# Five batches in the first class of early loads, one allocation for the load buffers, the places' products two steps later, and an adapter down-projection in four blocks

## The chip, the cores and the metric

The kernel runs on one core of a Trainium2 chip, in one launch. The metric is the device time of one execution in microseconds (us). Over 12 executions it was 346.51 us in the median, from 345.58 to 347.81 us. The engines are TensorE (PE in the profile; its weight loads are PEld), VectorE (DVE), ScalarE (ACT), GpSimd (POOL) and SyncE (SP, which here issues most of the DMAs; SPq is its queue).

## The reference

The input `x` has 8 batches of 256 tokens of 128 numbers, all in f32: 2048 tokens, or 16 tiles of 128. There are two layers, each with a residual.

```
# layer 0: a pooling as condition, then 8 experts, all of them computed for every token
scores = tanh(x @ W1 + b1) @ v
p      = softmax(scores masked by the batch's kind)      # up to j / from j / all but j
pooled = (p @ x) / cnt
logits = pooled @ gate_weight.T
gates  = logits * (logits >= the kth smallest of all logits)
x      = x + sum over e of gates[e] * (gelu_tanh(pooled @ w1[e].T + b1[e]) @ w2[e].T + b2[e])
# layer 1: an adapter chosen by the batch's language, then the 2 best of 8 experts
h      = relu(x @ W1[lang] + b1[lang])                   # 128 -> 32
z      = layernorm(x + h @ W2[lang] + b2[lang]) * gamma[lang] + beta[lang]
xn     = layernorm(z) * gamma + beta
w, idx = the two largest of softmax(xn @ gate_w), scaled to sum 1
x      = x + z + sum over the two of w * (gelu(xn @ w1[e] + b1[e]) @ w2[e] + b2[e])
```

## The kernel before

**Units.** The 16 token tiles are cut into five units: units 0 to 2 are full units of four tiles (two batches), units 3 and 4 are half units of two tiles (one batch each). `halves(u)` names the two batches of a full unit, and twice the same batch for a half unit.

**Loading.** SyncE issues, in this order: the input, the first layer's weights `w` (L147, 24 of 256 KB), then for each unit the adapter's weights in loads from L200 on: `lw1` (128 x 32), `lw2` (33 x 129: 32 rows of W2 and a row of b2, with b1 as column 129 of the 32 rows), and `lgb` (gamma and beta). A unit's two `lw2` lie in one tile `las[u]`, at partitions 0 and 64 (`LANE`).

**The pooling.** For batch b, TensorE multiplies the masked weights with the tokens, the gate's columns and a column of ones (`poolp`, L390). VectorE takes the row sums (`rs`, L397), their reciprocal (L398), `pooled` (L400) and the batch's `logit` out of it. Two batches together are turned on TensorE (`poolTp`, L407) and copied by VectorE to `poolT` (L409). Then the first layer's products can start. The order on each engine is settled when the program is built: a planner sorts the operations by its own costs and due times. Those of the beginning (up to L502, on TensorE, VectorE, ScalarE and GpSimd) and of the ending (from L1161, on SyncE too) keep the order of the text among themselves, but an operation from further down in the text may be placed between those of the beginning. A `keep_in_program_order` fixes a single instruction in the same way.

**The first layer.** `layer("first")` goes over the five units and the eight experts. For each, four products `hp_first` (L945) with a GELU on ScalarE each (L947), then, one expert later, four products `yp_first` (L925) into one PSUM tile; VectorE multiplies that with the gates (`part_first`, L913) and adds it up (`acc_first`, L915). Between these products `pump()` advances everything in `behind` by one step: the poolings that remain, the search of the kth value (`threshold`, L531 to L554), and for each finished unit the generator `adapt(u)`. A `yield` in a generator is one step: what follows it is emitted after the next product.

**`adapt(u)`** is the second layer's first half for one unit:

- `x2T`, the residual in turned form (L694); `fp`, the turn back on TensorE; `x` on VectorE (L698);
- `adp`, the down-projection (L705): one product of 32 x (half the unit's tokens) for each of the two lanes, of 256 columns in a full unit, of 128 in a half unit; VectorE adds b1 and takes the relu into `ha` (L707);
- `dp`, the up-projection (L715), one product per tile of 128 tokens, from the two lanes in turn; `xr` adds the residual (L720);
- two layer norms, with GpSimd's `rstd_l` (L582) in them; the turn `znp` (L749); the logits `l1q` and `l1p` (L763, L770, L775);
- the two best experts (`oh1`, `oh2`), the running counts of tokens per expert `sofar` (L802), two steps of pause, and then the places' products `kp` on TensorE (L808, L809), which count for each token its place in its expert's list;
- `at` (L814), the counts of the unit (L817), the counts of a class (`some`, L821), and the scatters of the tokens to DRAM `xs` by GpSimd (L830), then the list of tiles that are full by now.

**The second layer** runs over 36 tiles of 128 rows and, if needed, up to three more. `fetch` issues the loads of weights (`wt`, L983) and tokens (`xt`, L993) some tiles ahead, `turn` turns them (`xtp`, L1019, `xc`, L1021), `hidden` makes the hidden layer (`b`, L1031; `hps`, L1034; `hs`, L1036), `output` the products `yps` (L1043), `yt` (L1047), and scatters the outputs back by GpSimd to `ys` (L1050).

**Classes.** Tiles are taken in an order such that the batches' outputs are complete early for some: class one holds the first `FIRST` = 4 batches, class two those up to `EARLY` = 6. With k the number of a tile, `SETTLED_FIRST` = max(29, 4 x 4 + 7) = 29 and `SETTLED` = 31; at k = 28 `load` fetches the batches of the first class, `yg`, from `ys` (L1069), at k = 30 those of the second. The last two batches are loaded when the loop is over. `add()` adds a batch's two outputs into `resid` (L1076, L1077) and `store` writes it out (L1085). In the ending, three adds and stores stand between the outputs of the last tiles, one more after `brought`, and the rest after all. The outputs of the last four tiles don't go through DRAM: `home` (L1092 to L1099) makes a matrix of places and `brought` (L1106) multiplies it with the outputs into `late`, which VectorE adds at the end (L1182).

Of the kernel before, what the change touches and what calls it, by code (L numbers as in the profile page):

```python
# [10 lines left out]
F32 = mybir.dt.float32  # L11
# [3 lines left out]
ALU = mybir.AluOpType  # L15
# [7 lines left out]
B, S, D = 8, 256, 128  # L23
P = 128
NT = B * S // P
NG = 4
GT = NT // NG
# [3 lines left out]
NU = len(UNITS)  # L31
SLOTS = {2: 17, 3: 21, 4: 39}
E, HC = 8, 4
A = 32
LANE = 64
# [4 lines left out]
NSCR = 15  # L40
# [4 lines left out]
NSLOT = SLOTS[NU - 1]  # L45
SURE = 36
EARLY = 6
FIRST = 4
CLASSES = 3


SETTLED = max(SLOTS[NU - 2] + E, 4 * EARLY + E - 1)
SETTLED_FIRST = max(SLOTS[NU - 2] + E, 4 * FIRST + E - 1)

# [30 lines left out]
def halves(u):  # L85

    g, o, nt = UNITS[u]
    b = (g * GT + o) // 2
    return (b, b + 1) if nt == GT else (b, b)
# [3 lines left out]
def tile_adaln_ffn_d2(ctx: ExitStack, tc: tile.TileContext, x, ptype, lang, cols, b1v,  # L93
                      w10, w20, w11d, w21d, lw1, lw2, lgb, out):
    nc = tc.nc
# [3 lines left out]
    const = ctx.enter_context(tc.tile_pool(name="const", bufs=1))  # L99
    first = ctx.enter_context(tc.tile_pool(name="first", bufs=E))  # L100
    keep = ctx.enter_context(tc.tile_pool(name="keep", bufs=NG))
    work = ctx.enter_context(tc.tile_pool(name="work", bufs=2))
    small = ctx.enter_context(tc.tile_pool(name="small", bufs=4))
    dram = ctx.enter_context(tc.tile_pool(name="dram", bufs=1, space=DRAM))
    psb = ctx.enter_context(tc.tile_pool(name="psb", bufs=4, space=PSUM))
# [36 lines left out]
    for e in range(E):  # L142
        t = first.tile([P, HC * P], F32, tag="w1", name=f"w10_{e}")
        nc.sync.dma_start(out=t, in_=w10[e])
        w10s.append(t)
        t = first.tile([P, HC, D], F32, tag="w2", name=f"w20_{e}")
# [16 lines left out]
    for i, (sign, keeps) in enumerate(((-1, ALU.is_ge), (1, ALU.is_ge), (1, ALU.not_equal))):  # L163
# [25 lines left out]
    lws, las, lgs = [], [], []  # L189
    langs = [nc.values_load(lgi[0:1, b:b + 1], engines=(SP,), min_val=0, max_val=NL - 1,  # L190
                            skip_runtime_bounds_check_because="a language's number") for b in range(B)]
    for u, (g, o, nt) in enumerate(UNITS):
        la = const.tile([LANE + A + 1, D + 1], F32, name=f"lw2_{u}")
        las.append(la)
        for i, b in enumerate(halves(u)):
            if nt == GT or not i:
                t = const.tile([P, A], F32, name=f"lw1_{b}")
                nc.sync.dma_start(out=t, in_=lw1[bass.ds(langs[b] * P, P), :])
                lws.append(t)
            nc.sync.dma_start(out=la[i * LANE:i * LANE + A + 1, :], in_=lw2[bass.ds(langs[b] * (A + 1), A + 1), :])  # L200
            if nt == GT or not i:
                t = const.tile([P, 2 * D], F32, name=f"lgb_{b}")
                nc.sync.dma_start(out=t, in_=lgb[bass.ds(langs[b], 1), :].rearrange("o w -> (o w)").partition_broadcast(P))
                lgs.append(t)
# [131 lines left out]
    for g in range(NG):  # L336
        nc.tensor.matmul(slp[:, g], lhsT=inner[g], rhs=vw[:, :, :2],
                         start=True, stop=True)
# [23 lines left out]
    for i in range(2):  # L362
        for g in range(NG):
            quadrant = slice(g * A, (g + 1) * A)
            nc.tensor.matmul(tops[2 * g + i], lhsT=ident[quadrant, g * A + i:g * A + i + 1].to_broadcast([A, P]),
                             rhs=top[quadrant, :], start=True, stop=True)
# [123 lines left out]
    while known < half + 1:  # L490
        n = min(known, half + 1 - known)
# [135 lines left out]
    for e in range(E):  # L627
        nc.sync.dma_start(out=w21[:, e, :], in_=w21d[e].rearrange("p c d -> p (c d)"))
    nc.sync.dma_start(out=b2all.rearrange("p e d -> p (e d)"),
                      in_=b2d.rearrange("e d -> (e d)").partition_broadcast(P))  # L630
    for n in range(EARLY, B):
        nc.sync.dma_start(out=ys[n * 4 * P:(n + 1) * 4 * P, :].rearrange("(p t) d -> p t d", t=GT), in_=empty[:, :, :D])
    rows = xs.rearrange("(p m t) c -> p m (t c)", p=P, t=GT)
# [12 lines left out]
    def tiles_of(counts, edges, name, f=None):  # L646

        c2 = small.tile([P, E, NT], F32, tag="c2", name=f"c2_{name}", bufs=1)
        nc.vector.tensor_tensor(c2, counts.unsqueeze(2).to_broadcast([P, E, NT]),
                                edges.unsqueeze(1).to_broadcast([P, E, NT]), ALU.is_ge)  # L650
        if f is None:
            f = small.tile([P, E], F32, tag="f", name=f"nf_{name}", bufs=2)
        nc.vector.tensor_reduce(f, c2, AX.X, ALU.add)  # L653
        return f
# [34 lines left out]
    def adapt(u, acc):  # L689
        g, o, nt = UNITS[u]  # L690
        n, t0 = nt * P, g * GT + o
        batches = range(t0 // 2, (t0 + nt) // 2)
        x2T = work.tile([P, GN], F32, tag="x2T", name=f"x2T{u}")[:, :n]
        nc.vector.tensor_tensor(x2T, acc, xT[g][:, o * P:o * P + n], ALU.add)  # L694
        yield
# [3 lines left out]
        yield  # L699

        m, lanes = n // 2, [slice(0, A), slice(LANE, LANE + A)]
        hp = psb.tile([LANE + A, S], F32, tag="big", name=f"adp{u}")[:, :m]
        ha = has[u % 2][:, :m]
        for i, b in enumerate(halves(u)):
            nc.tensor.matmul(hp[lanes[i], :], lhsT=lws[b], rhs=x2T[:, i * m:(i + 1) * m], start=True, stop=True)  # L705
        for lane in lanes:
            nc.vector.tensor_scalar(ha[lane, :], hp[lane, :], las[u][lane, D:D + 1], 0.0, ALU.add, ALU.max)  # L707
        yield
        yield

        dps = [psb.tile([P, 2, D], F32, tag="big", name=f"dp{u}_{i}") for i in range(2)]
        for t in range(nt // 2):
            for i, lane in enumerate(lanes):
                rows = slice(lane.start, lane.stop + 1)
                nc.tensor.matmul(dps[i][:, t, :], lhsT=ha[rows, t * P:(t + 1) * P], rhs=las[u][rows, :D],  # L715
                                 start=True, stop=True)
        z = work.tile([P, GT, D], F32, tag="xr", name=f"xr{u}")[:, :nt, :]
        for i in range(2):
            part = slice(i * nt // 2, (i + 1) * nt // 2)
# [39 lines left out]
        if nt == GT:  # L759

            lq = pss.tile([P, P], F32, tag="sm", name=f"l1q{u}")
            for t in range(nt):
                nc.tensor.matmul(lq[t * A:(t + 1) * A, :], lhsT=col[:, C_G1:C_G1 + A], rhs=zt[:, t * P:(t + 1) * P],  # L763
                                 start=True, stop=True)
# [7 lines left out]
        else:  # L772
            lp = pss.tile([P, GT, E], F32, tag="sm", name=f"l1p{u}")[:, :nt, :]
            for t in range(nt):
                nc.tensor.matmul(lp[:, t, :], lhsT=zt[:, t * P:(t + 1) * P], rhs=col[:, C_G1:C_G1 + E],  # L775
                                 start=True, stop=True)
# [26 lines left out]
        last[0] = sofar[:, nt, :]  # L803
        yield
        yield
        kp = pss.tile([P, GT + 1, E], F32, tag="sm", name=f"kp{u}")[:, :nt + 1, :]
        flat = kp.rearrange("p t e -> p (t e)")
        nc.tensor.matmul(flat, lhsT=one16, rhs=sofar.rearrange("p t e -> p (t e)"), start=True, stop=False)  # L808
# [6 lines left out]
        if u in SLOTS:  # L815
            counts = small.tile([P, E], F32, tag="counts", name=f"counts{u}", bufs=2)
            nc.vector.tensor_copy(counts, kp[:, nt, :])  # L817
        for i, n0 in enumerate((FIRST, EARLY)):
            if t0 + nt == 2 * n0:
                some = small.tile([P, E], F32, tag="some", name=f"some{i}", bufs=1)  # L820
                nc.vector.tensor_copy(some, kp[:, nt, :])  # L821
                tiles_of(some, begun, f"some{i}", holding[:, i, :])
        for s, oh in enumerate((oh1, oh2)):
            wh = small.tile([P, GT, E], F32, tag="s", name=f"wh{u}_{s}")[:, :nt, :]
# [4 lines left out]
            for t in range(nt):  # L829
                move = nc.gpsimd.indirect_dma_start(  # L830
                    out=xs, out_offset=bass.IndirectOffsetOnAxis(ap=pos[:, t:t + 1], axis=0),
                    in_=zr[s][:, t, :], in_offset=None)
# [8 lines left out]
        if u in SLOTS:  # L841

            k0, k1 = SLOTS.get(u - 1, 0), SLOTS[u]
            f = tiles_of(counts, begun if u == NU - 1 else full, str(u))
# [194 lines left out]
    def output(k, xt, hT, b2):  # L1039
# [14 lines left out]
        tc.add_to_no_dep_group("outputs", move.ins)  # L1054
        for settled, n0, n1 in ((SETTLED_FIRST, 0, FIRST), (SETTLED, FIRST, EARLY)):
            if k >= settled:
# [7 lines left out]
    of = out.rearrange("b (p u) d -> b p u d", u=2)  # L1064
    loaded = deque()

    def load(n, part, queue, group=None):
        y = work.tile([P, 2, 2 * D], F32, tag="scr", name=f"yg{n}_{part.start}", bufs=NSCR)[:, part, :]
        move = queue.dma_start(out=y, in_=yv[n, :, part, :])  # L1069
        if group:  # L1070
            tc.add_to_no_dep_group(group, move.ins)
        loaded.append((n, part, y))

    def add():
        n, part, y, o = taken_up()
        nc.vector.tensor_tensor(o, y[:, :, :D], o, ALU.add)  # L1076
        nc.vector.tensor_tensor(o, o, y[:, :, D:], ALU.add)  # L1077
        return n, o

    def taken_up():  # L1080
        n, part, y = loaded.popleft()
        return n, part, y, resid[n // 2][:, n % 2 * 2:n % 2 * 2 + 2, :]

    def store(queue, n, o):
        queue.dma_start(out=of[n], in_=o)  # L1085
# [17 lines left out]
    def brought(k, yt, sums, begin, ends=0):  # L1103

        for i in range(GT):
            nc.tensor.matmul(sums[i // 2][:, i % 2, :], lhsT=homes[k][:, i * P:(i + 1) * P], rhs=yt,  # L1106
                             start=begin and i % 2 == 0, stop=i // 2 < ends and i % 2 == 1)
# [20 lines left out]
    def early():  # L1128
        for k in range(LEAD + PRIMED):
            ahead(k)  # L1130
        for _ in range(PRIMED):
            flipped.append(turn(*fetched.popleft()))

    behind.append(run("poolings", poolings()))
    behind.append(run("threshold", threshold()))
    layer("first", AF.Gelu_apprx_tanh, poolT, w10s, w20s, C_B10, C_B20, gates0, "pool", adapt,
          early)

# [24 lines left out]
    for n in range(EARLY, B):  # L1163
        load(n, slice(0, 2), nc.sync)
# [6 lines left out]
    store(nc.sync, *add())  # L1171
    placed.append(output(*hid.popleft()))
    brought(*placed[0], late, True)
    store(nc.sync, *add())
    placed.append(output(*hid.popleft()))
    for k in range(1, SURE - PLACED):
        brought(*placed[k], late, False, LATE * (k == SURE - PLACED - 1))
    for _ in range(FIRST, EARLY):
        store(nc.sync, *add())
# [62 lines left out]
```

## Time and profile before

| What | Value |
|---|---|
| median of 12 executions | 346.51 us (345.58 to 347.81) |
| profiled execution, its own time | 346.24 us |
| its span, first to last instruction | 344.5 us |
| mean granted TensorE clock | 0.996 of full |
| TensorE busy | 336.2 us, 98% of the span |
| VectorE busy | 197.4 us, 57% |
| ScalarE busy | 170.6 us, 50% |
| GpSimd busy | 93.5 us, 27% |
| `yp_first` (L925) | 320 products, 120.2 us |
| `hp_first` (L945) | 320 products, 119.8 us |
| moved by DMA | 47.56 MB, 138 GB/s in the mean |

The profiled execution's own time is 1.7 us more than its span: that lies ahead of the first and behind the last instruction. Matmuls are pipelined and their ends are modelled, so a share of 98% for TensorE says that there is nearly always a product under way, not that each goes at its peak. The time of an order or a window is counted from the first instruction. "a\*b" behind a product's tiles is the size of its weights, then follow the shape and type of its output, and "xN" counts equal instructions in a row.

### The profile page before, as it was taken

How to read it: one execution, taken by the hardware profiler on the slowest of the kernel's cores; microseconds unless marked ns; L12 is line 12 of the kernel's file. 1: busy time of each engine (PE TensorE's matmuls, PEld its weight loads, DVE VectorE, ACT ScalarE, POOL GpSimd, SP SyncE). 2: the span in 40 equal slices, each digit the busy share in tenths (PEclk: the TensorE clock that was granted, in tenths of full speed). 3: DMA queues.
4: the chain of work that ended last, by engine and by line, in shares of the span. 5: the costliest groups of instructions: out<-in, count | busy, mean ns of one | idle time of the engine just before them, and what ended most of it. 6: DMA issues, size and time to landing. Idle time of an engine off the chain costs nothing. (4 is left out here: it accounts for less than half of the span.)

```text
span 344.5 us, 6117 instructions
## 1 busy us (share of the span) xinstructions
PE 336.2 (98%) x1662; PEld 221.8 (64%) x1662; DVE 197.4 (57%) x835; ACT 170.6 (50%) x393; POOL 93.5 (27%) x146
## 2 busy tenths in 40 slices
PE   8999999999999999999999999999999999999993
PEld 7785444444444444444444568877887999999993
DVE  2884766542234585757361347569768668733474
ACT  3575345543443333323533434544467678778660
POOL 6600000000000031174027001206504565765520
PEclk9999999999999999999999999999999999999998
DMA  7882699935214201021112011112376575588465
GB/s 197 289 298 72 173 370 381 381 131 157 65 62 142 73 30 30 30 86 39 62 38 62 23 30 32 43 35 72 89 198 169 168 215 156 158 226 230 123 199 186
DMA packets 35771, 47.56 MB, mean 138 GB/s; under 512 B 5449, under 2 KB 18588, under 8 KB 35736
## 3 DMA queue, kind: packets, MB, share of 16 engines
q1 hardware_dynamic: 32744, 42.17, 40.3%
q0 software_dynamic: 2144, 4.19, 3.6%
q10 hardware_dynamic: 848, 0.79, 0.8%
q8 instruction: 15, 0.25, 0.3%
q14 instruction: 20, 0.16, 0.2%
HBM read 32.66 MB, written 14.66 MB: 137 GB/s over the span
## 5 line engine op out<-in xcount | busy, mean ns | idle before, releaser
L947 ACT ACTIVATE hT_first<-hp_first,col 128x512 f32<-128x512 f32 (+1 forms) x160 | 93.2, 601 | 91.5 <-PE hp_first L945 90.4
L925 PE MATMUL yp_first<-hT_first,w 128*128 128x512 f32 (+1 forms) x320 | 120.2, 513 | 0.0
L945 PE MATMUL hp_first<-poolT,w 128*128 128x512 f32 (+1 forms) x320 | 119.8, 512 | 0.0
L925 PEld LDWEIGHTS yp_first<-hT_first,w 128*128 128x128 f32 x320 | 58.8, 191 | 45.2 <-issue 40.9
L945 PEld LDWEIGHTS hp_first<-poolT,w 128*128 128x128 f32 x320 | 58.8, 190 | 44.4 <-issue 39.7
L830 POOL DMA_INDIRECT xs<-zr,pos x32 | 32.5, 1015 | 67.7 <-DVE holding L653 32.9
L1036 ACT ACTIVATE hs<-hps,col 128x128 f32<-128x128 f32 x144 | 40.6, 375 | 11.8 <-PE hps L1034 8.4
L913 DVE SCALAR_TENSOR_TENSOR part_first<-yp_first,col,gbc_first 128x512 f32<-128x512 f32 (+1 forms) x28 | 17.2, 614 | 39.6 <-PE yp_first L925 39.4
L1043 PE MATMUL yps<-w,hs 128*128 x288 | 38.3, 277 | 0.5 <-ACT hs L1036 0.4
L1050 POOL DMA_INDIRECT ys<-yt,xt x32 | 31.9, 997 | 24.4 <-DVE yt L1047 14.8
L1034 PE MATMUL hps<-xc,wt 128*128 128x128 f32 x288 | 38.2, 276 | 0.0
L1043 PEld LDWEIGHTS yps<-w,hs 128*128 128x128 f32 x288 | 35.0, 192 | 1.1 <-issue 0.8
L1034 PEld LDWEIGHTS hps<-xc,wt 128*128 128x128 f32 x288 | 35.1, 192 | 0.4 <-issue 0.2
L582 POOL TENSOR_TENSOR rstd_l<-ve_l,nhalf 128x4 f32<-128x4 f32 (+1 forms) x5 | 5.0, 1005 | 69.4 <-DVE ve_l L580 69.3
L1047 DVE SCALAR_TENSOR_TENSOR yt<-yps,xt,b 128x128 f32<-128x128 f32 x36 | 12.5, 348 | 18.4 <-PE yps L1043 18.3
L915 DVE TENSOR_TENSOR acc_first<-acc_first,part_first 128x512 f32<-128x512 f32 (+1 forms) x35 | 20.1, 581 | 0.5
L1021 ACT ACTIVATE xc<-xtp,col 128x128 f32<-128x128 f32 x36 | 16.7, 470 | 7.2 <-PE xtp L1019 7.0
L516 POOL DMA_DIRECT2D gd_L<-gT_L x1 | 0.7, 655 | 61.1 <-DVE gT_L L514 61.1
L933 ACT ACTIVATE y_first<-yp_first,col 128x512 f32<-128x512 f32 x8 | 5.5, 687 | 23.2 <-PE yp_first L925 14.6
L1031 DVE TENSOR_TENSOR b<-b2all,xt 128x128 f32<-128x128 f32 x36 | 10.4, 290 | 7.8 <-DVE yt L1047 3.7
L531 DVE TENSOR_SCALAR_CACHE_REDUCE fl<-logit,tr 128x128 bf16<-128x128 f32 x46 | 13.5, 343 | 0.6
L550 DVE TENSOR_SCALAR_CACHE_REDUCE ok<-kt 128x3 f32<-128x3 f32 (+1 forms) x16 | 2.6, 161 | 13.8 <-PE kt L534 13.8
(253 smaller groups left out, 302.8 us busy)
## 6 DMA issues: line engine op xcount, KB each, us to landing
wt<-in_w_dram SPq DMA_DIRECT2D x36, 256.0 KB
xs<-empty SPq DMA_DIRECT2D x1, 8580.0 KB
w<-in_w_dram SPq DMA_DIRECT2D x24, 256.0 KB
gbc_first<-gd_L SPq DMA_DIRECT2D x24, 256.0 KB
xt<-xs SPq DMA_DIRECT2D x36, 65.0 KB
gbc_first<-gd_L SPq DMA_DIRECT2D x16, 128.0 KB
yg<-ys SPq DMA_DIRECT2D x8, 256.0 KB
xg<-in_x_dram SPq DMA_DIRECT2D x8, 128.0 KB
```

What stands on the lines that cost most here:

```text
L531: nc.vector.tensor_scalar(flags, lflat, values[:, i:i + 1], None, ALU.is_lt, ALU.add, accum_out=c[:, i:i + 1])
L830: move = nc.gpsimd.indirect_dma_start(out=xs, out_offset=bass.IndirectOffsetOnAxis(ap=pos[:, t:t + 1], axis=0), in_=zr[s][:, t, :], in_off ...
L913: nc.vector.scalar_tensor_tensor(part, y, bias, gbc, ALU.add, ALU.mult)
L915: nc.vector.tensor_tensor(accs[u], accs[u], part, ALU.add)
L925: nc.tensor.matmul(yp, lhsT=w2s[e][:, c, :], rhs=hT[:, c, :], start=(c == 0), stop=(c == HC - 1))
L945: nc.tensor.matmul(hp, lhsT=w1s[e][:, c * P:(c + 1) * P], rhs=sources[g][:, o * P:o * P + n], start=True, stop=True)
L947: nc.scalar.activation(hT[:, c, :], hp, act, bias=col[:, cb1 + e * HC + c:cb1 + e * HC + c + 1])
L1021: nc.scalar.activation(xc, tp, AF.Identity, bias=col[:, C_LB:C_LB + 1], scale=col[:, C_LG:C_LG + 1])
L1034: nc.tensor.matmul(hp[:, c, :], lhsT=wt[:, c * P:(c + 1) * P], rhs=xc, start=True, stop=True)
L1036: nc.scalar.activation(hT[:, c, :], hp[:, c, :], AF.Gelu, bias=b1all[:, bass.ds(number(k, ACT), 1), c])
L1043: nc.tensor.matmul(yp, lhsT=hT[:, c, :], rhs=w21[:, bass.ds(ek, 1), c * D:(c + 1) * D], start=(c == 0), stop=(c == HC - 1))
L1050: move = nc.gpsimd.indirect_dma_start(out=ys, out_offset=bass.IndirectOffsetOnAxis(ap=xt.bitcast(I32)[:, D:D + 1], axis=0), in_=yt, in_off ...
```

## The change

- `FIRST` becomes 5: the first class holds five batches, so five loads are issued where four were, at k = 28 (`SETTLED_FIRST` = max(29, 4 x 5 + 7) stays 29), and the second class one. In the ending, `FIRST - 3`, now two, adds stand after `brought`, and one after all. The counts of a class are now taken from the unit in which its last batch lies, also in its middle: both classes' in unit 2.
- The load buffers of all eight batches are allocated together at the first load.
- In full units two more steps of pause stand ahead of `kp`.
- In full units the down-projection `adp` goes in four products of 128 columns, one per tile, each into 32 partitions of its own; the bias and relu go in four steps. Since the second and fourth block lie at partitions 32 to 63 and 96 to 127, the b1 column is copied there by two VectorE copies per full unit, into a column that `las` gets in addition; they stand at the top of `adapt(u)`, in the text.
- The products of `dp` go from lane 1 to lane 0; the second product of a pair is pinned behind the first (`tc.keep_in_program_order`), and in the last unit both; the same is done for `adp` of the half units.

```diff
-FIRST = 4
+FIRST = 5
...
-        la = const.tile([LANE + A + 1, D + 1], F32, name=f"lw2_{u}")
+        la = const.tile([P, D + 2], F32, name=f"lw2_{u}")
...
-            nc.sync.dma_start(out=la[i * LANE:i * LANE + A + 1, :], in_=lw2[bass.ds(langs[b] * (A + 1), A + 1), :])
+            nc.sync.dma_start(out=la[i * LANE:i * LANE + A + 1, :D + 1], in_=lw2[bass.ds(langs[b] * (A + 1), A + 1), :])
...
+        if nt == GT:
+            for i in (0, LANE):
+                nc.vector.tensor_copy(las[u][i + A:i + 2 * A, D + 1:], las[u][i:i + A, D:D + 1])
         x2T = work.tile([P, GN], F32, tag="x2T", name=f"x2T{u}")[:, :n]
...
-        hp = psb.tile([LANE + A, S], F32, tag="big", name=f"adp{u}")[:, :m]
+        hp = psb.tile([P, S], F32, tag="big", name=f"adp{u}")
         ha = has[u % 2][:, :m]
-        for i, b in enumerate(halves(u)):
-            nc.tensor.matmul(hp[lanes[i], :], lhsT=lws[b], rhs=x2T[:, i * m:(i + 1) * m], start=True, stop=True)
-        for lane in lanes:
-            nc.vector.tensor_scalar(ha[lane, :], hp[lane, :], las[u][lane, D:D + 1], 0.0, ALU.add, ALU.max)
+        if nt == GT:
+            for q in range(GT):
+                nc.tensor.matmul(hp[q * A:(q + 1) * A, :P], lhsT=lws[halves(u)[q // 2]], rhs=x2T[:, q * P:(q + 1) * P],
+                                 start=True, stop=True)
+            for q in range(GT):
+                i, j, quarter = q // 2, q % 2, slice(q * A, (q + 1) * A)
+                nc.vector.tensor_scalar(ha[lanes[i], j * P:(j + 1) * P], hp[quarter, :P],
+                                        las[u][quarter, D + j:D + j + 1], 0.0, ALU.add, ALU.max)
+        else:
+            for i, b in enumerate(halves(u)):
+                move = nc.tensor.matmul(hp[lanes[i], :m], lhsT=lws[b], rhs=x2T[:, i * m:(i + 1) * m],
+                                        start=True, stop=True)
+                if i or u == NU - 1:
+                    tc.keep_in_program_order(move)
+            for lane in lanes:
+                nc.vector.tensor_scalar(ha[lane, :], hp[lane, :m], las[u][lane, D:D + 1], 0.0, ALU.add, ALU.max)
...
-            for i, lane in enumerate(lanes):
-                rows = slice(lane.start, lane.stop + 1)
-                nc.tensor.matmul(dps[i][:, t, :], lhsT=ha[rows, t * P:(t + 1) * P], rhs=las[u][rows, :D],
-                                 start=True, stop=True)
+            for i in (1, 0):
+                rows = slice(lanes[i].start, lanes[i].stop + 1)
+                move = nc.tensor.matmul(dps[i][:, t, :], lhsT=ha[rows, t * P:(t + 1) * P], rhs=las[u][rows, :D],
+                                        start=True, stop=True)
+                if not i or u == NU - 1:
+                    tc.keep_in_program_order(move)
...
         last[0] = sofar[:, nt, :]
         yield
         yield
+        if nt == GT:
+            yield
+            yield
         kp = pss.tile([P, GT + 1, E], F32, tag="sm", name=f"kp{u}")[:, :nt + 1, :]
...
-            if t0 + nt == 2 * n0:
+            if t0 < 2 * n0 <= t0 + nt:
                 some = small.tile([P, E], F32, tag="some", name=f"some{i}", bufs=1)
-                nc.vector.tensor_copy(some, kp[:, nt, :])
+                nc.vector.tensor_copy(some, kp[:, 2 * n0 - t0, :])
...
+    brought_back = []
+
     def load(n, part, queue, group=None):
-        y = work.tile([P, 2, 2 * D], F32, tag="scr", name=f"yg{n}_{part.start}", bufs=NSCR)[:, part, :]
+        if not brought_back:
+            brought_back.extend(work.tile([P, 2, 2 * D], F32, tag="scr", name=f"yg{m}", bufs=NSCR) for m in range(B))
+        y = brought_back[n][:, part, :]
...
-    store(nc.sync, *add())
+    for _ in range(FIRST - 3):
+        store(nc.sync, *add())
     placed.append(output(*hid.popleft()))
...
```

## The prediction

> **What bounds the kernel now.** I read the page's busy shares and chain of waits first, then windows of 1 us, then the engines' order of time around each edit.
>
> ```profile
> PE 336.2 (98%) x1662; PEld 221.8 (64%) x1662; DVE 197.4 (57%) x835; ACT 170.6 (50%) x393; POOL 93.5 (27%) x146
> ...
> PE 19%; DVE 2%; DMA 1%; issue 0%; ACT 0%; DVEq 0%
> ```
>
> TensorE is busy from 1 to 339 us with some 2 us of gaps, so up to 339 us a microsecond that it waits or saves is a microsecond of the span; after that the tail counts (last adds, stores). A stall of another engine matters if TensorE's next instruction needs it. That is read from the order of time. First the pooling of the batches, TensorE and then VectorE (start, duration, engine, line, operation, tiles, sizes, count):
>
> ```profile
> 15.75 5.87 PE L390 MATMUL poolp<-xg,probs 128*128 128x137 f32 x48
> 21.46 0.60 PE L407 MATMUL poolTp<-ident,pooled 128*128 128x128 f32 x4
> ...
> 22.94 1.02 PE L945 MATMUL hp_first<-poolT,w 128*128 128x512 f32 x2
> ```
>
> ```profile
> 19.00 0.15 DVE L397 TENSOR_TENSOR rs<-poolp,cnt 128x2 f32<-128x2 f32 x1
> 19.18 0.17 DVE L398 RECIPROCAL rs<-rs 128x2 f32<-128x2 f32 x1
> ...
> 20.19 0.42 DVE L400 TENSOR_TENSOR pooled<-poolp,rs 128x256 f32<-128x256 f32 x1
> ...
> 22.09 0.69 DVE L409 COPY poolT<-poolTp 128x512 f32<-128x512 f32 x1 [1.39 <-PE poolTp L407]
> ```
>
> TensorE finds both `pooled` tiles there (20.6 us) when it turns them at 21.46, and `hp_first` can start once `poolT` is copied. Nothing else is queued for TensorE before: six poolings are done, the seventh stands behind the turn.
>
> **The change, part by part. 1: the copies of `lw2`.** The diff adds, per full unit, two 32x1 copies of the adapter's bias column, six in all. Their own time is small (the 128x8 copy of L821 takes 0.16 us; six are 1 us at most). But they wait for the loads of `lw2`, and the built program's order, compared with the one of before, puts them into the pooling on VectorE:
>
> ```
> rs(batch 0); copy lw2 unit 0; reciprocal; pooled 0; logit; rs 1; reciprocal;
> copy lw2 unit 0; pooled 1; logit; poolT 0; rs 4; copy unit 1; ... pooled 4; rs 5;
> ... copy unit 1; pooled 5; ... rs 7; pooled 2; pooled 3; reciprocal;
> copy unit 2; copy unit 2; pooled 7; logit; first count of the search; poolT 1
> ```
>
> The loads come late on SyncE's queue, behind 4 MB of first-layer weights (order of time on SyncE, then windows of 1 us):
>
> ```profile
> 18.68 0.33 SPq L147 DMA_DIRECT2D w<-in_w_dram  x1
> ...
> 20.33 0.36 SPq L200 DMA_DIRECT2D lw<-in_lw_dram  x1
> ...
> 31.71 0.35 SPq L200 DMA_DIRECT2D lw<-in_lw_dram  x1
> ```
>
> ```profile
> 22.00:23.00 1.00, 1.00 (x11) 0.97 (x10) 0.87 (x3) 0.00 (x0) 0.00 (x0) 1.00 1.06 382
> 23.00:24.00 1.00, 1.00 (x5) 0.52 (x5) 0.93 (x7) 0.00 (x0) 0.00 (x0) 1.00 0.74 207
> ```
>
> The next-to-last column of a window is the DMA share: the engines are full until 23 us. The trace's records of semaphores agree: the six loads that the copies wait for raise theirs for the last time at 25.31, 26.01, 26.56, 28.52, 31.58 and 33.28 us. VectorE runs in order, so behind the first copy are queued the reciprocal and both `pooled`: they move from 19.2 to 25.4 us. With the spacing of the rows above (reciprocal 0.2, `pooled` 0.4, logit 0.1, `rs` 0.2), `pooled 1` is ready at about 26.9, the turn ends at 27.25, `poolT 0` at 28.1, and `hp_first` starts at 28.4: 5.4 us later. The sixth copy waits until 33.3, `pooled 7` and its logit end at 34.05; TensorE reaches the turn that needs that PSUM slot at 34.1. So this adds next to nothing: 5.5 us of stall. Its bounds: 4.5 if the loads land 1 us earlier, 6.5 if 1 us later.
>
> **The clock.** TensorE then idles from 21.5 to 26.2 us, but for two turns to 27. In the tail it ends at 339.14:
>
> ```profile
> 341.50:342.00 0.50, 0.00 (x0) 0.00 (x0) 0.00 (x0) 0.00 (x0) 0.00 (x0) 0.86 0.98 338
> 342.00:342.50 0.50, 0.00 (x0) 0.00 (x0) 0.00 (x0) 0.00 (x0) 0.00 (x0) 0.50 0.35 117
> ```
>
> The granted clock (third column from the right) falls to half 2.7 us after the last matmul; a gap of 4.7 us should do it. At the start the clock record turns full at 7.35 us, 6.2 us after the first matmul at 1.13. Half speed for 3.4 to 6.2 us of work from 27 us on costs half of that, 1.7 to 3.1 us; none if the clock holds. I take 2.2, nearer to the lower end since the trace's two changes lie 98 steps of 3.41 us apart, and that grid here gives 24.4 to 31.2 (2.0). The Trainium skill ("TensorE: Matmul & The Clock Gate", Part 1) speaks of such free-running windows of about 3.4 us and asks for a whole idle one before the clock halves; the tail's 2.7 us is shorter than that. By that rule a gap of 4.7 us would halve the clock in only some 4 of 10 positions of the window, and the sum would stay near 350.
>
> The skill's page "DMA: Bandwidth & Descriptors" (Anatomy of one DMA) gives about 2 us of fixed cost for a transfer; the first load here took 5.0 from issue, as it stands behind the weights. By the page the copies would pass at 22.3 and 24.5, and the stall would be about 3.5 us, the time near 349 or 350.
>
> **2: places' products two steps later.** Removed are these waits of TensorE (total us, times, longest):
>
> ```profile
> PE kp L808 <- DVE sofar L802: 0.7, 2, 0.3
> ```
>
> of units 0 and 1: in the new order two matmuls of 0.43 to 0.86 us more stand between, so -0.7. For unit 2 there was no wait; its list comes about 1 us later, which the nine or so us between the first tile's load (247.4) and its turn (260.1) hide. VectorE now also computes both classes' counts in that unit (0.7 us), within the same cover. Unit 3 runs behind unit 2 in the same queue of steps, and its `kp` falls from 257.8 to behind the last `yp_first_6`, 260.1, with only 3.5 us from `l1p`: I expect a wait of 0.3 there, and VectorE's chain (full at 259 to 266 us) lets unit 4's `fp`, which needs its last sum, start 1.5 us later than now, of which the gaps around it already hold most. Unit 4's paired `dp` gives back 0.4. Together +0.3, bounds -0.7 and +1.5.
>
> **3: four blocks, pairs pinned.** The order of time on TensorE around `adp`, then around unit 3's `dp`:
>
> ```profile
> 117.38 0.62 PE L705 MATMUL adp<-x2T,lw 128*32 128x256 f32 x4
> 117.94 1.98 PE L925 MATMUL yp_first<-hT_first,w 128*128 128x512 f32 x4
> ```
>
> ```profile
> 238.99 0.49 PE L715 MATMUL dp<-lw,ha 33*128 33x128 f32 x2
> 239.41 0.70 PE L925 MATMUL yp_first<-hT_first,w 128*128 128x256 f32 x2
> 240.04 0.49 PE L715 MATMUL dp<-lw,ha 33*128 33x128 f32 x2
> ```
>
> Two 256-wide products take 0.56 us start to start; four blocks of the same form as `l1q` (eight passes, 137.44 to 137.79) take 0.35: -0.2 each for three units, -0.6 (0 if they do not overlap). VectorE's two bias steps of 0.47 become four of 0.34, +0.4 us, hidden by the 1.7 us of `yp_first` or `hp_first` before `dp`. In unit 3 the halves of `dp` take 0.42 and 0.41 apart, with 0.2 lost on the return between; as a pair about 0.43: -0.5.
>
> **4: fifth batch in the first class.** `SETTLED_FIRST` stays 29, so the five loads go where four went, and one load fewer stands in the last burst. From the chain of waits, near its end:
>
> ```profile
> 333.89 4.56 DMA yg<-ys
> ...
> 338.47 0.43 DVE resid L1076
> ```
>
> Now VectorE adds batches 4 and 5 up to 338.45, when batch 6 lands. Without batch 4's add (0.8) and its 256 KB (0.9 us at the 290 GB/s of that stretch), both move up; next is TensorE's last `late` at 339.0. I take -0.7 (bounds 0, if the fifth load holds up the last outputs' writes, and -0.9). Allocating the load buffers together takes no wait away: in both orders the loads wait on ACT, PE and the outputs' writes.
>
> **Sum.** 5.5 + 2.2 - 0.7 + 0.3 - 0.6 - 0.5 - 0.7 = +5.5. The profiled execution has a span of 344.5 and took 346.24; that gives 351.7, and 352.0 from the median of 346.51. A difference below 0.2% (0.7 us) is no difference for this kernel's measurement.
>
> **Rivals.** (a) The clock holds or halves only briefly: 5.5 - 2.2 = +3.3, 349.8. For: the gap is broken by two turns at 26.2. Against: the tail's 2.7 us. (b) The gains do not come: the waits of `kp` go over to `fp` (+1.5), the tail stays: 7.7 + 1.5 - 0.7 - 0.6 - 0.5 = +7.4, 353.9. For: VectorE is busy 9.0 of the 10 us from 260. (c) Faster: the copies at the pooling pass without a wait, because the loads' data are there, and the rest remains: -2.2, 344.3. It decides if the first two copies pass before 21 us; up to about 22.5 the change would still not be slower. Against it stand an issue at 20.33 and full DMA engines until 23.
>
> **Chances.** Forecast 0.5, (a) 0.27, (b) 0.13, (c) 0.10. Range 348.7 to 354.4: from (a) with 1 us less stall to (b) with half a microsecond more; outside are (c) and some of the edges. Faster 0.09 and same 0.02 come from (c), slower 0.89 from the rest.
>
> **What would show it.** VectorE idle before the copies of L695 for about 6 us near 19 to 25, released by a DMA; `hp_first` from 28 us; a granted clock of half somewhere in 24 to 32; no wait of `kp` in units 0 and 1; `adp` of 0.35 us; the `dp` pairs together; one add pair fewer before the last. If `hp_first` starts before 24 us, I am wrong.

## The result and the profile after

The changed kernel takes 351.96 us in the median of 11 executions (351.19 to 353.26). The kernel before took 346.13 us over 46 executions (345.33 to 348.14). The ratio is 1.0162, with a 95% interval of 1.0148 to 1.0177: it is slower by 5.6 us (by the two medians 5.8). The profiled execution has a span of 350.2 us against 344.5.

The loss lies at the start. VectorE's order of time in the profile after, at the place that the prediction showed for before:

```profile
19.00 0.15 DVE L397 TENSOR_TENSOR rs<-poolp,cnt 128x2 f32<-128x2 f32 x1
26.17 0.14 DVE L695 COPY lw<-lw 32x1 f32<-32x1 f32 x1 [7.03 <-DMA lw<-in_lw_dram]
26.35 0.17 DVE L398 RECIPROCAL rs<-rs 128x2 f32<-128x2 f32 x1
...
28.74 0.69 DVE L409 COPY poolT<-poolTp 128x512 f32<-128x512 f32 x1 [0.69 <-PE poolTp L407]
```

Between `rs` and its reciprocal, 0.03 us apart before, stands a copy of 0.14 us that waited 7.03 us for its load. TensorE's order of time shows what that held up:

```profile
27.21 1.49 PE L407 MATMUL poolTp<-ident,pooled 128*128 128x128 f32 x4 [5.59 <-DVE rs L397]
...
30.54 1.91 PE L965 MATMUL hp_first<-poolT,w 128*128 128x512 f32 x2
```

The turn names `rs` as what it waited for; what held it up is the copy that stands behind the first `rs` on VectorE. The first `hp_first` comes at 30.54, 7.6 us later than before, and takes 1.91 us for two products instead of 1.02. The windows of 1 us say why (third column from the right is the granted clock):

```profile
22.00:23.00 1.00, 0.00 (x0) 0.00 (x0) 0.00 (x0) 0.00 (x0) 0.00 (x0) 1.00 1.03 381
26.00:27.00 1.00, 0.00 (x0) 0.00 (x0) 0.76 (x5) 0.00 (x0) 0.00 (x0) 0.50 0.32 92
30.00:31.00 1.00, 1.00 (x5) 0.77 (x4) 0.69 (x5) 0.00 (x0) 0.00 (x0) 0.50 0.53 82
33.00:34.00 1.00, 1.00 (x6) 0.66 (x6) 0.52 (x4) 0.99 (x2) 0.00 (x0) 1.00 0.39 93
```

In the clock's own record it is half from 25.61 to 32.44 us.

To see where the rest goes I compare the start of the n-th product of a name in both traces. From the second expert on, the first layer is 8.5 us late. That shrinks to 6.1 behind unit 3's `dp` (247 us of the old time), is 6.4 at 271 us, 6.1 at the last `late`, and 5.7 at the end of the span. The steps of the shrinkage are visible in TensorE's order of time, here `adp` of unit 0 and `dp` of unit 3:

```profile
125.91 0.42 PE L709 MATMUL adp<-x2T,lw 128*32 128x128 f32 x8
126.27 1.98 PE L945 MATMUL yp_first<-hT_first,w 128*128 128x512 f32 x4
...
247.38 0.49 PE L730 MATMUL dp<-lw,ha 33*128 33x128 f32 x4
247.80 1.56 PE L965 MATMUL hp_first<-poolT,w 128*128 128x256 f32 x6
```

`adp` takes 0.36 us from start to start (0.56 before), and unit 3's four passes of `dp` stand together. The list of TensorE's waits has no `kp` any more, and a new line:

```profile
PE fp L566 <- DVE acc_first L935: 1.2, 1, 1.2
```

### The profile page after: what moved, and what is told of

The parts are those of the page before. It is cut to its first block, busy times and chain, and to the rows that moved or that the text cites. A ratio compares the mean times of both kernels' runs of the same rounds, so it can differ in the third digit from the quotient of the medians.

```text
span 350.2 us, 6149 instructions
## 1 busy us (share of the span) xinstructions
PE 335.0 (96%) x1674; PEld 222.3 (63%) x1674; DVE 199.8 (57%) x847; ACT 170.9 (49%) x393; POOL 92.2 (26%) x146
## 5 line engine op out<-in xcount | busy, mean ns | idle before, releaser
L850 POOL DMA_INDIRECT xs<-zr,pos x32 | 31.7, 990 | 70.4 <-DVE pos L848 33.1
L1067 DVE SCALAR_TENSOR_TENSOR yt<-yps,xt,b 128x128 f32<-128x128 f32 x36 | 12.5, 348 | 15.1 <-PE yps L1063 15.0
```

The lines of the kernel that those rows point to most:

```text
L850: move = nc.gpsimd.indirect_dma_start(out=xs, out_offset=bass.IndirectOffsetOnAxis(ap=pos[:, t:t + 1], axis=0), in_=zr[s][:, t, :], in_off ...
```

## The experiments

They ran in three sets; each ratio is against the kernel before in the same set, which took 352.83 us in the first set (e1 to e4), where second layers were slower, 346.47 us in the second (e5 to e8) and 346.17 us in the third (e9 to e12).

### e1 and e7: the copies pinned where the text has them

```diff
-                nc.vector.tensor_copy(las[u][i + A:i + 2 * A, D + 1:], las[u][i:i + A, D:D + 1])
+                tc.keep_in_program_order(
+                    nc.vector.tensor_copy(las[u][i + A:i + 2 * A, D + 1:], las[u][i:i + A, D:D + 1]))
```

> The changed kernel with one edit: the six copies of the bias column are pinned where the text has them, ahead of x2T in adapt(u), so VectorE meets them about 90 us after their loads. Theory 1 (the wait of the copies and the half clock after it are the whole loss): the first hp_first starts near 23 us again, the granted clock has no half at 25 to 32 us, and the 8.5 us by which the changed kernel's first-layer products are late go: 352.0 - 8.5 = 343.5 us, 2.6 below the kernel before. Theory 2 (the later edits cost too, the gains are not there): 346 us or more.

> The changed kernel with the copies pinned in adapt(u), on this chip. Theory 1: 8.5 us below the changed kernel and 2.6 below the kernel before. Theory 3, from e1 (the later places' products push back the lists and so the second layer's first loads, which then come too late): the first layer 2 us early at unit 3's end, and all of that and more lost between 250 and 285 us; 0 to 2 us over the kernel before.

In e7 the kernel takes 343.83 us, ratio 0.9929 (0.991 to 0.9948): 2.64 us faster than before, and 8.2 faster than the changed kernel of the same set (e5, 352.05). VectorE meets the copies at 116 us, without a wait, and the first `hp_first` is where it was:

```profile
116.03 0.32 DVE L695 COPY lw<-lw 32x1 f32<-32x1 f32 x2
```

```profile
22.78 1.02 PE L965 MATMUL hp_first<-poolT,w 128*128 128x512 f32 x2
```

So in this set the whole loss is the place of six copies of 0.15 us, and the rest of the change is worth 2.6 us. In e1, in the first set, the same kernel took 354.62 us, ratio 1.0054 (1.0025 to 1.0082): 1.8 us more than the kernel before, where theory 1 had 2.6 less. Its first `hp_first` starts at 23.53, the stall is gone there as well, and at 238 us of the old time it is 2.4 us ahead of its own start, as e7 is. Against e7 it then loses 1.8 us between 240 and 244 us, and 9.6 more from 264 to 324 us, though the same instructions stand in the same order in both. It isn't this kernel alone: e4, of the same set, loses 7.2 us against e10, the same kernel in the third set, 4.8 of them near 295 us. There TensorE stops inside a tile, for nothing that the profile names, and VectorE stands still for 3.23 us until 299.00:

```profile
294.98 0.83 PE L1034 MATMUL hps<-xc,wt 128*128 128x128 f32 x6
296.07 0.34 PE L1034 MATMUL hps<-xc,wt 128*128 128x128 f32 x1 [0.25 <-issue]
297.50 0.27 PE L1034 MATMUL hps<-xc,wt 128*128 128x128 f32 x1 [1.09 <-issue]
299.50 2.01 PE L1043 MATMUL yps<-w,hs 128*128 x8 [1.72 <-ACT xc L1021]
```

e1 and e2 have the like near their 300 us, and the traces of the later sets don't. Six products of the same tile had run, so a weight tile that lands late doesn't fit. In all four traces of the first set ScalarE, too, stands still for 2.7 to 4.0 us before one and the same `hs`, and the list of the last tiles (`rows`) comes 12.5 us after the last unit's `kp`; in the other ten it comes 9.1 to 9.3 us after it. What stopped the engines in that set is open. Theory 3, which I formed from e1, that the later places' products bring this about, fell with e7 and e8: with them the kernel is faster, and e4, which doesn't have them, stops as well.

### e2: the copies alone

```diff
+        if nt == GT:
+            for i in (0, LANE):
+                nc.vector.tensor_copy(las[u][i + A:i + 2 * A, D + 1:], las[u][i:i + A, D:D + 1])
```

(With the wider `las` tile, on the kernel before. e7 has the wider tile too, without a loss, so it isn't the tile.)

> The kernel before with the wider lw2 tile and the six copies alone, not pinned; nothing reads them. Theory 1: the start of the changed kernel without its gains; first hp_first near 30.5 us, half clock for two windows, +8.5 us: 354.6 us. Theory 2 (copies harmless by themselves): within 0.7 us of 346.1.

Ratio 1.024 (1.0202 to 1.0278), 8.8 us over the kernel before of that set; in the trace the first `hp_first` starts at 29.89 and the first layer runs 8.5 us late from the second expert to its end. The copies alone make the loss, as expected (8.5).

### e3 and e6: TensorE kept busy during the wait

```diff
-        for jt in range(2):
+        for jt in list(range(2)) * (6 if b == 5 else 1):
```

> The changed kernel, copies as they are; the products of the sixth pooling on TensorE are done six times instead of once (40 more passes of about 0.12 us, same result), so TensorE works from 21.6 to about 26.5 us while VectorE waits. Theory 1 (wait and clock are two terms): the clock stays full, the first hp_first comes at about 29, the changed kernel loses 2.6 us less: 349.4 us. Rival (the wait alone counts, the half clock hides under other waits of that stretch): 352.0 us within 0.7.

e3 missed: ratio 1.0453 (1.0405 to 1.0501), 16.4 us over the kernel before of its set. The added products changed the planner's order, and VectorE got more copies ahead of `poolT`:

```profile
29.74 0.15 DVE L695 COPY lw<-lw 32x1 f32<-32x1 f32 x1 [1.81 <-DMA lw<-in_lw_dram]
32.54 0.14 DVE L695 COPY lw<-lw 32x1 f32<-32x1 f32 x1 [2.65 <-DMA lw<-in_lw_dram]
32.71 0.69 DVE L409 COPY poolT<-poolTp 128x512 f32<-128x512 f32 x1
```

As a test of the clock it says nothing; it shows that how long the wait lasts depends on which copy the planner puts ahead of what. e6 writes the copies into `scaled()` at the places of the changed kernel, pinned:

```diff
         nc.vector.tensor_tensor(rs, pp[:, :, XW - 1], cnt[:, :, b], ALU.mult)
+        if b in (0, 4):
+            column(b // 4, 0)
         nc.vector.reciprocal(rs, rs)
+        if b in (1, 5):
+            column(b // 4, LANE)
+        if b == 7:
+            column(2, 0)
+            column(2, LANE)
```

> The changed kernel again, as the partner of the next three on one chip. First-layer products 8.5 us late once the clock is full; 5.8 us over the kernel before, if the second layer finds the same loads as in its first profile; up to 9 over it, if the second layer loses what the first experiments lost there.

> The changed kernel with the six copies written into the pooling at the very places where the planner had put them, and the products of the sixth pooling on TensorE done six times: the order on every engine is that of the changed kernel but for the 20 added products, so that the copies of units 1 and 2 do not come ahead of poolT as in e3. Theory 1 (wait and clock are two terms): full clock throughout, first hp_first near 29, the first layer 5.9 us late and not 8.5, total 2.6 us below the changed kernel. Rival (half clock hidden under other waits): same as the changed kernel within 0.7 us.

e5, the changed kernel, took 352.05 us, ratio 1.0167 (1.0135 to 1.0199); e6 took 351.31, ratio 1.0149 (1.0122 to 1.0176). In e6 the window at 30 us, half before, has a full clock:

```profile
30.00:31.00 1.00, 1.00 (x8) 0.76 (x8) 0.95 (x7) 0.51 (x1) 0.00 (x0) 1.00 0.31 91
```

The load landed at different times: the first copy passes at 26.24 in e6, at 26.17 in the first profile of the changed kernel, at 25.09 in e5. With equal landing, e6 against the first profile, the first layer is 7.0 late and not 8.5: the half clock costs 1.5 us, the wait 7.0. By the medians it is 0.7, inside the overlap of the intervals, so the times alone don't exclude the rival. The traces have two terms, the clock's smaller than the 2.6 expected: in e6 TensorE waits 0.3 us at a turn (35.55 us) for the last of the copies, a wait that the half clock had hidden. The split rests on one pair of profiles.

### e8, e9 and e12: the later places' products

e8 is e7 without the two added yields; e9 is the kernel before with them alone; e12 is e7 with the condition `if u < 2:` in place of `if nt == GT:`.

> As the last one, but the places' products where the kernel before has them (no added yields). Theory 3: the loss of e1 between 250 and 285 us goes; at the last late the kernel is 1.1 us ahead of the kernel before by the four blocks and the pairs, and the tail gives up to 0.7: 1.1 to 1.8 us below the kernel before, and below the kernel with the later products. Theory 1 as predicted (later products gain 0.4 net): 0.4 us slower than that kernel.

> The kernel before with the two added yields ahead of kp in full units, nothing else. As predicted: 0.7 less in units 0 and 1, 0.3 more at units 3 and 4, together 0.4 below the kernel before. From the traces of e7 and e8 (0.5 less at each of units 0 and 1, 0.3 less at unit 2, 0.4 more between 250 and 270 us): 0.9 below. From their times (343.83 against 345.62): 1.8 below.

> The kernel of e7 with the two added yields in units 0 and 1 alone, so that units 2 and 3 have kp where the kernel before has it. If the later products of unit 2 only push work into the stretch from 250 to 270 us, this one is 0.1 to 0.5 below e7; if they gain there too (a wait of TensorE at unit 2's kp, lists that are not needed so early), it is 0.2 to 0.8 above e7.

| | time, us | ratio to before | interval |
|---|---|---|---|
| e7, with them | 343.83 | 0.9929 | 0.991 to 0.9948 |
| e8, without | 345.62 | 0.9974 | 0.9958 to 0.999 |
| e9, they alone | 345.33 | 0.9972 | 0.9944 to 0.9999 |
| e12, units 0 and 1 | 345.05 | 0.9958 | 0.9933 to 0.9983 |

They gain in every comparison of times: 1.8 us beside the other edits, where the prediction had 0.4; 0.8 alone, with an interval that begins at nothing. e12 stands 1.1 below its kernel before, e7 2.6 below its own. So unit 2's later products seem to gain too, and more than the 0.2 to 0.8 expected; but the intervals overlap, and the two ran in different sets. By the traces each of units 0 and 1 gains 0.5 us and unit 2 gains 0.3. (e8's profile is of its slowest execution, 348.53 us, so its trace serves here up to unit 3 only.) In e9 the first layer is 1.9 us ahead of its own start at 257 us of the old time (the planner paired unit 3's `dp` by itself there), and all of it is lost again by 271, where TensorE waits at unit 4's `fp`:

```profile
263.28 0.41 PE L566 MATMUL fp<-ident,acc_first 128*128 128x128 f32 x2 [1.38 <-DVE cf L643]
264.13 0.41 PE L705 MATMUL adp<-x2T,lw 128*32 128x128 f32 x2 [0.45 <-DVE x2T L694]
```

In e7 the same stretch costs 0.3. Which of the other edits makes that difference wasn't separated.

### e4 and e10: five batches in the first class

> The kernel before with FIRST = 5, the class counts inside a unit, the extra add ahead of the last output and the load buffers together; nothing else. By the prediction the tail is 0.7 us shorter: 345.4 us against 346.1. By the changed kernel's trace, whose tail from the last late to the end is 0.4 shorter: 345.7. Rival (the last loads wait for the last outputs anyway): 346.1.

> The kernel before with the fifth batch in the first class, as in e4. As predicted 0.7 below the kernel before; by the changed kernel's trace 0.4 below; the rival of e4: no difference.

e4: 353.05 us, ratio 1.001 (0.9987 to 1.0033). e10: 346.26, ratio 0.9987 (0.9965 to 1.0008). No difference is seen; e10's interval alone would still hold the 0.7 that was predicted, e4's doesn't. The tail speaks against it as well. From the last `late` product to the end of the span it is 5.67, 5.37 and 5.41 us with `FIRST` = 4 (before, e9, e11), and with 5 it is 5.31, 5.78, 5.81, 5.57, 5.77, 5.77 and 5.97 (after, e5, e6, e7, e8, e10, e12). The first set spreads more: 6.59 with 4 (e2), 4.88, 6.08 and 5.75 with 5 (e1, e3, e4). One end of the chain of waits, in e10:

```profile
334.97 3.36 DMA yg<-ys
...
338.35 0.44 DVE resid L1080
...
338.81 0.42 DVE resid L1081
```

VectorE has added the batches before and waits 0.39 us for the last load. SyncE issues the last burst of loads only behind GpSimd's last scatter to `ys`: the scatter's instruction ends at 332.40 and the burst begins at 332.99 in the profile before, at 332.07 and 332.87 in e10. The last load of all is issued at 335.18 and 334.97. Taking batch 4's load out of this burst moves neither, which is what e4's rival said.

### e11: four blocks and pairs

> The kernel before with the down-projection in four blocks, the copies for it pinned in adapt(u), and the pinned pairs of dp and of the half units' adp; FIRST and kp as before. As predicted: 0.6 by the blocks and 0.5 by unit 3's pair, 1.1 below the kernel before, and nothing from unit 4's pair; by e8's trace 1.2 below until unit 3's end.

345.51 us, ratio 0.9973 (0.9948 to 0.9998). In the trace the lead over its own start is 0.6 us by the blocks and 1.2 with unit 3's pair, both as expected; 1.0 is left at the last `late`. (The first `hp_first` starts 0.7 us earlier to 1.4 later than in the profile before, in kernels that change nothing ahead of it; so leads are counted from there.) By ratios, e9, e10 and e11 alone give 0.28 + 0.13 + 0.27 = 0.68%, e7 together 0.71%: the parts add up, as far as intervals of 0.2 to 0.3% to each side can tell.

## Why the prediction was right, and where its steps were not

The number (352.0 for 351.96) and its main step hold: the copies wait in the pooling (e2), without that wait the change is faster (e7, 343.83, where rival (c) had 344.3), and TensorE meets no other large loss. That the number is exact is partly luck, as terms missed both ways:

- **The stall** was put at 5.5 us with a landing at 25.3. In e5, with 25.09, the first layer is 7.8 late with the clock's part in it, near the 7.7 of the sum. The first profile after had 26.17, as SyncE issued the load at 22.07 and not at 20.33. With the clock held (e6) the stall alone is 7.0: 0.9 of it the later landing and 0.5 the last two copies' turn, which the prediction held for next to nothing.
- **The clock** halved as said, for two windows; it was put at 2.2 and measured 1.5 (profile against e6; by medians 0.7). The Trainium skill ("TensorE: Matmul & The Clock Gate", Part 1) has the clock halve after a whole idle window of about 3.4 us; here the window from 22.20 to 25.61 was idle, and the half clock lasted 6.83 us, two windows. Row and rule agree in this place; the last section has places where they don't.
- **The loads.** The Trainium skill's "DMA: Bandwidth & Descriptors" (Anatomy of one DMA), with about 2 us of fixed cost, gave a stall of 3.5 us. In the five traces with copies in the pooling the first one passes 3.9 to 5.1 us after its load's issue (4.1 in the first profile after, issued at 22.07). No run has 2 us there. That section is written for transfers that GpSimd issues; these are issued by SyncE, behind 4 MB of weights (16 of the 24 loads of `w`; the other eight come later, from 38 us on). How much of the time is the queue in front wasn't measured apart.
- **The places' products** were mis-sized: -0.7 + 0.3 was predicted, the trace has -1.3 by the end of unit 3 and +0.4 after it, the times -0.8 to -1.8. A wait of 0.34 us on TensorE costs 0.5: in unit 0, from the start of the product before `kp` to the start of the one behind, it is 0.99 us in the profile before and 0.48 in e7. Unit 2's `kp`, said to have no wait, waited 0.07 us, below what the list shows, and cost 0.25 (0.52 us against 0.27). (From the load of the first tile, 247.4, to its turn, 260.1, it is 12.7 us and not nine: the cover was larger than the prediction read.) The wait at `fp` that was foreseen is there (1.2 us), and as foreseen the gaps around it held most of it.
- **Blocks and pair**: -0.6 and -0.5 predicted; -0.6 and -0.6 in the traces.
- **The tail** failed: -0.7 predicted, nothing found. The step that "both move up" without batch 4's add and load was wrong, since the last loads wait for the last scatter to `ys` and aren't moved by them. The 0.4 that the first profile after shows lies inside the tail's spread.

Sum of the first profile's traces: 8.5 - 0.6 - 1.3 - 0.6 + 0.4 - 0.3 - 0.4 = 5.7, which is the difference of the spans; the -0.3 lies between 271 us and the last `late`, and no edit was found for it.

## What to carry to other kernels

Where a planner orders the instructions, look up in the built order where each small new operation landed and which load it waits for: an in-order engine turns a copy of 0.15 us into a stall of 7 us of everything behind it. Pin it next to its use, and the same change gains 0.7% (e7; not in e1, in the set with the slower second layers). An edit at the end is worth something only if it moves the load that comes last.

## What the runs showed of the hardware

The clock halves also after windows that are not idle. Its changes lie on a grid of 3.41 us. In the fourteen profiles, every window of that grid at full clock in which TensorE's modelled busy time was at most 0.45 of it was followed by half clock (22 windows); the least busy that was not had 0.49. Above that there is no clean line: between 0.49 and 0.65, fourteen were not and three were. Eleven of the 22 had no product at all. The tail that the prediction went by is one of the others: its window, 338.44 to 341.86 us in the profile before, was busy for 0.20 of it. An example from e4, a window with three products and the next one:

```profile
296.10:299.50 3.40, 0.59 (x3) 0.27 (x3) 0.50 (x3) 0.87 (x4) 1.58 (x2) 1.00 0.14 44
299.50:303.00 3.50, 3.50 (x17) 3.50 (x18) 2.92 (x16) 2.76 (x10) 2.05 (x3) 0.51 0.36 108
```

Busy 0.59 of 3.40 us, and the next window runs at half. SyncE's pace behind the large loads also varied more than expected: with the same order of issues the first `lw2` was issued between 20.31 and 22.46 us over the fourteen traces, and the first copy in the pooling passed between 25.09 and 26.24.
